# New statement order in the written-out front and end of a cross-attention layer on one core

## The chip, the cores and the metric

The kernel runs on one core of one Trainium2 chip. A core has five engines with an instruction queue each: TensorE (PE in the profile, its weight loads PEld), VectorE (DVE), ScalarE (ACT), GpSimd (POOL) and SyncE (SP), which issues most transfers. Each engine works through its own instructions in the order in which the program gives them, and waits where an operand or a buffer is not there yet. The metric is the device time of one execution in microseconds (us); lower is better.

## The reference

One transformer layer: 16-head cross attention of `x` (128 x 128 x 256) to a context of the same shape, a feed-forward part of width 1024 with relu, and a layer norm behind each. The mask is strict (`j < i`), and row 0 of the weights is set to 0.

```python
q = (query @ Wq + bq).reshape(b, s, N_HEADS, D_K).transpose(0, 2, 1, 3)
k = (key @ Wk + bk).reshape(b, s, N_HEADS, D_K).transpose(0, 2, 1, 3)
v = (values @ Wv + bv).reshape(b, s, N_HEADS, D_K).transpose(0, 2, 1, 3)
scores = jnp.einsum('bhqd,bhkd->bhqk', q, k) / jnp.sqrt(jnp.float32(D_K))
scores = jnp.where(allowed, scores, NEG_INF)
attn = jax.nn.softmax(scores, axis=-1)
attn = attn.at[:, :, 0, :].set(0.0)
ctx = jnp.einsum('bhqk,bhkd->bhqd', attn, v).transpose(0, 2, 1, 3).reshape(b, s, d)
x = layer_norm(query + ctx @ Wo + bo, ln1_g, ln1_b)
ffn = jax.nn.relu(x @ W1 + b1) @ W2 + b2
out = layer_norm(x + ffn, ln2_g, ln2_b)
```

## The kernel before

The 128 sequences are worked in 64 pairs, p = 0 to 63, 256 rows each. The order on every engine is that of the statements: a manual schedule, with no planner behind it. There are three parts:

- **The front**, lines 1863 to 2449: pairs 0 to 6 by statements of their own, then steps 7 and 8 with the keys of the regular step, written out one by one as `do("weigh", 8)` and so on.
- **The regular step**, line 2450: `for p in range(9, 61): step(p)`, 52 steps over one list of keys, `ORDER` (each key one small operation, some for an older pair), with `EMPTY` naming where PE is given empty instructions.
- **The end**, line 2453 on: steps 61 and 62 written out with the same keys, and a tail for pair 63 and all that is still open of 59 to 63.

A step interleaves several pairs: the scores and softmax of p, the projections of the next, the attention output of p-2 and the feed-forward part of p-3 and p-4. Large products are made from seven block products instead of eight; for that, `combine_weights` (L1105 to L1108, four POOL instructions) makes sums of weight blocks once (`wvt`, `wot`, `wqt`, `wkt`), and for the hidden layer of the last pairs `late(p).run(n)` (class `Hidden`, L1050) makes product n, with `xS` (POOL, L1646) the sums of its input's blocks.

Names that the steps below use:

- `mask` (L456, L464), `maximum` (DVE L475, then POOL L476 subtracts), `exponential` (ACT L483, in the regular step `eh`/`el` keys, L937), `sums` (DVE L498/L499, then POOL L500 normalises): the softmax, by high (`hi` = 1) and low half of the rows.
- `turn_on_pe` (PE L569, ACT L571) and `turn` with `bring_all` (DVE L533, then transfers L552): the weights turned for the product with the values, in the first pairs on PE, later by DVE and sixteen small transfers. `weigh` (PE L586, L596) is that product, `context` and `attention_out` (L635) follow it; `attention_sum` (DVE L683) adds the input, to which `add_bo` (POOL L295) has added a bias.
- `project_keys`, `project_queries` (PE L300), `copy_keys` (ACT L345); in the regular step queries and keys leave PSUM at ACT L1181 and L1219, values at L1265, L1278 and L1695.
- `hidden`, `second`, `second_sum` (DVE L904), `second_product` (L977), `sum_add` (L995): the feed-forward part. `residual1` (POOL L721, L724) prepares what `second_sum` adds.
- In the tail `scale_62` (DVE L1809) and `shift_62` (L1816, which needs POOL's deviation of L657/L658) make the output of pair 62; `last_part` (PE L1826, DVE L1834/L1835 or L1832), `last_scale` (L1839, L1840, POOL L1841), `last_shift` (L1845) and `last_out` (L1852, then a store) that of pair 63.

PSUM has eight banks, used by number, so a product can also wait for a bank to be read out.

Of the kernel before, what the change touches and what calls it, by code (L numbers as in the profile page):

```python
# [10 lines left out]
ALU = mybir.AluOpType  # L11
# [8 lines left out]
def tile_cross_attention_block(  # L20
# [1877 lines left out]
    mask(1, 1, B)  # L1898
    project_keys(2)
    add_bo(0)  # L1900
# [4 lines left out]
    maximum(1, 1, ONE)  # L1905
    scores(1, 0)
    exponential(1, 1, ONE)
    weigh(0)
    context(0)
    project_queries(2)  # L1910
    maximum(1, 1, TWO)
    mask(1, 0, A)
    mask(1, 0, B)
    maximum(1, 0, ALL)
    attention_out(0)
    copy_keys(2)
    exponential(1, 1, TWO)
    values(2)
    sums(1, 1, ONE)
    tokens(3, "c")  # L1920
    copy_queries(2)
    exponential(1, 0, ALL)
    scores(2, 1)
    attention_sum(0)
    stats(0, states[0]["t1"], 1)
    deviation(0, 1)
    stack_values(2)
    shift(0, 1)
# [21 lines left out]
    turn_on_pe(1, 1, range(3, 4))  # L1950
    tokens(3, "x")
    mask(2, 0, B)
    turn_on_pe(1, 0, range(0, 1))
    mask(2, 0, A)
    add_bo(1)
    maximum(2, 0, ALL)
# [44 lines left out]
    exponential(3, 1, TWO)  # L2001
    mask(3, 0, A)
    maximum(3, 0, ALL)
    second(0, 1)
    weigh(2)
    spread_values(3)
    context(2)
    second_sum(0)
    project_keys(4, 6)
    sums(3, 1, ONE)  # L2010
    exponential(3, 0, ALL)
    attention_out(2)
    scale_w1()
    copy_keys(4)
    sums(3, 1, TWO)
    sums(3, 0, ALL)
    project_queries(4)
    attention_sum(2)
# [31 lines left out]
    project_keys(5)  # L2050
    maximum(4, 1, TWO)
    exponential(4, 0, ALL)
    sums(4, 1, ONE)
    exponential(4, 1, TWO)
    sums(4, 0, ALL)
    sums(4, 1, TWO)
    second(1, 1)
    second_sum(1)
    hidden(2, range(2, 4), None, (2, 3, 4, 0))
    residual1(2)  # L2060
    turn(4, 0, 0)
    load_ahead(3)
    copy_keys(5)
    copy_queries(5)
# [12 lines left out]
    tokens(6, "c")
    mask_high(5, 2, 2)
    exponential_by_head(5, 1, range(8, 12), True)
    exponential_by_head(5, 1, range(12, 16), True)  # L2080
    mask(5, 0, A)
    project_queries(6)
    mask(5, 0, B)
    bring(4, nc.sync, LATE_FIRST)
    low_maximum(5)
    exponential_by_head(5, 0, range(8, 12), True)
    mask_high(5, 0, 1)
# [1015 lines left out]
```

## Time and profile before

| | us |
|---|---|
| runs | 1472.11, 1468.98, 1474.38; median 1472.11 |
| the profiled execution | 1469.98 |
| its span, first to last instruction | 1468.2 |
| mean granted TensorE clock | 0.997 |

All durations below come from the profiled execution. A line of its timeline has the start, the duration, the engine, the line of the kernel, the operation, output <- input and a count of equal instructions, and in brackets the idle time before it with what released it. Two numbers of PE overlap a little, since matmuls are pipelined; what a group takes is best read from its start to the start of the next.

### The profile page before, as it was taken

To read this page: it belongs to the slowest core of one execution; us is meant where nothing else is said; L and a number is where in the kernel's file an instruction comes from. 1 tells how busy PE (TensorE), PEld (TensorE's weight loads), DVE (VectorE), ACT (ScalarE), POOL (GpSimd) and SP (SyncE) were. 2 spreads that over 40 slices of the span, in tenths; PEclk is the share of its full clock that TensorE was granted. 3 is DMA by queue.
4 is the path that set the end of the run, shared out by engine and by line. 5 is a ranking of instruction groups with operands and counts; after the bars stand their busy time and mean duration, and the time that the engine had idled before them with its cause. 6 is when DMAs were issued, how large, how long until landed. Compare 5 with 4: busy or idle time off the path is not lost.

```text
span 1468.2 us, 62017 instructions
## 1 busy us (share of the span) xinstructions
PE 1447.0 (99%) x20713; PEld 1391.6 (95%) x20713; DVE 1371.9 (93%) x3175; ACT 1303.4 (89%) x5559; POOL 1271.2 (87%) x1872
## 2 busy tenths in 40 slices
PE   8999899999999999999999999999999999999998
PEld 7778799999999999999999999999999999999988
DVE  6987999999999999999999999999999999999767
ACT  5659899999999999999999999999999999999743
POOL 5986898988988988988988998998998998998966
PEclk9999999999999999999999999999999999999999
DMA  8274766766766766766766766766766776774541
GB/s 208 63 143 102 179 154 156 162 157 156 161 160 153 162 158 153 163 160 153 160 158 157 159 158 158 160 158 156 163 157 153 163 161 149 164 158 116 140 103 51
DMA packets 367881, 220.34 MB, mean 150 GB/s; under 512 B 280032, under 2 KB 335584, under 8 KB 367584
## 3 DMA queue, kind: packets, MB, share of 16 engines
q1 hardware_dynamic: 365296, 214.27, 63.8%
q8 instruction: 187, 3.06, 1.0%
q10 hardware_dynamic: 2288, 2.11, 0.7%
q14 instruction: 110, 0.90, 0.2%
HBM read 55.06 MB, written 18.09 MB: 50 GB/s over the span
## 4 chain that ended last, share of the span: by engine, by line
PE 92%; DVE 4%; POOL 1%; DMA 1%; ACT 1%; issue 1%; SPq 0%; DVEq 0%; ACTq 0%; POOLq 0%
PE banks L1153 48%; PE banks L1364 24%; PE banks L440 6%; PE banks L596 4%; PE banks L586 2%; PE banks L300 2%; PE banks L875 2%; PE banks L977 1%; PE banks L635 1%; PE banks L356 1%; DVE sm L464 1%; ACT sm L937 1%; DVE turned L533 1%; PE banks L1050 0%; PE banks L1412 0%
## 5 line engine op out<-in xcount | busy, mean ns | idle before, releaser
L937 ACT ACTIVATE sm<-banks,nmx 128x128 f32<-128x128 f32 x944 | 340.8, 396 | 17.9 <-DVE nmx L1568 14.7
L937 ACT ACTIVATE sm<-sm,nmx 128x64 f32<-128x64 f32 x944 | 325.2, 384 | 1.5 <-DVE nmx L926 1.5
L937 ACT ACTIVATION_READ_ACCUMULATOR sm<-banks,nmx 128x1 f32 x944 | 222.8, 236 | 0.0
L937 ACT ACTIVATION_READ_ACCUMULATOR sm<-sm,nmx 128x1 f32 x944 | 221.8, 235 | 0.0
L533 DVE STREAM_TRANSPOSE turned<-sm 128x1024 f32<-128x1024 f32 x186 | 217.0, 1214 | 3.3 <-DMA brought<-turned 1.8
L1153 PE MATMUL banks<-wt,hS 128*128 128x128 f32 x1344 | 177.7, 275 | 0.0
L1364 PE MATMUL banks<-xS,w1t 128*128 128x128 f32 x1344 | 177.2, 275 | 0.0
L1153 PEld LDWEIGHTS banks<-wt,hS 128*128 128x128 f32 x1344 | 163.6, 192 | 0.1
L1364 PEld LDWEIGHTS banks<-xS,w1t 128*128 128x128 f32 x1344 | 163.4, 192 | 0.0
L1568 DVE TENSOR_REDUCE nmx<-banks 128x4 f32<-128x512 f32 x224 | 152.3, 680 | 1.9
L1557 POOL TENSOR_TENSOR hS<-hT 128x512 f32<-128x512 f32 x116 | 148.2, 1279 | 3.7 <-ACT hT L882 2.4
L1364 PE MATMUL banks<-brought,w 128*128 128x128 f32 x896 | 118.2, 275 | 0.0
L1153 PE MATMUL banks<-w,hT 128*128 128x128 f32 x896 | 109.8, 275 | 0.0
L1364 PEld LDWEIGHTS banks<-brought,w 128*128 128x128 f32 x896 | 109.0, 192 | 0.0
L1618 POOL TENSOR_TENSOR x1b<-x,g_r 128x512 f32<-128x512 f32 x56 | 72.4, 1293 | 39.4 <-ACT x L709 39.4
L1153 PEld LDWEIGHTS banks<-w,hT 128*128 128x128 f32 x896 | 104.8, 192 | 0.1
L440 PE MATMUL banks<-kT,qT 32*64 32x128 f32 (+1 forms) x3840 | 98.3, 331 | 1.8 <-ACT vz L1278 1.5
L1393 ACT ACTIVATE hT<-hT,b1e_c 128x256 f32<-128x256 f32 x224 | 95.7, 510 | 1.2 <-DVE hT L1389 1.1
L1562 DVE TENSOR_TENSOR banks<-banks,neg 128x256 f32<-128x256 f32 x224 | 93.3, 417 | 0.0
L440 PEld LDWEIGHTS banks<-kT,qT 32*64 32x64 f32 x3840 | 79.4, 131 | 12.6 <-ACT vz L1278 1.9
L709 ACT ACTIVATE x<-t,nb,sd 128x256 f32<-128x256 f32 x126 | 68.4, 593 | 19.7 <-POOL nb L732 12.9
L1219 ACT ACTIVATE kr<-banks,b_c 128x128 f32<-128x128 f32 x224 | 83.7, 411 | 1.7 <-PE banks L1153 1.7
(324 smaller groups left out, 4821.5 us busy)
## 6 DMA issues: line engine op xcount, KB each, us to landing
brought<-turned SPq DMA_DIRECT2D x936, 128.0 KB, 2.4
out_dram<-t SPq DMA_DIRECT2D x63, 256.0 KB, 4.0
xb<-in_x_dram SPq DMA_DIRECT2D x124, 128.0 KB, 3.2
cb<-in_ctx_dram SPq DMA_DIRECT2D x124, 128.0 KB, 3.2
x<-in_x_dram SPq DMA_DIRECT2D x56, 256.0 KB, 2.8
kT<-kr SPq DMA_DIRECT2D x112, 128.0 KB, 2.2
brought<-turned SPq DMA_DIRECT2D x40, 96.0 KB, 2.4
w<-in_L_xattn_W_dram SPq DMA_DIRECT2D x2, 1024.0 KB, 7.4
```

Of the source, the lines that this page charges most:

```text
L440: nc.tensor.matmul(st["sps", hi][r][s * HP : (s + 1) * HP, m * 2 * n : (m + 1) * 2 * n].rearrange("p (e j) -> p e j", e=2), st["qT"][strip ...
L533: nc.vector.transpose(turned[:, :, at : at + 256].rearrange("p j (n a) -> p n j a", a=32), states[p]["sm", hi].rearrange("p h j -> p (h j) ...
L709: nc.scalar.activation(x1[:, s], t1[:, s], AF.Identity, bias=st["nb", 1][:, s], scale=sd[:, s])
L937: nc.scalar.activation(sm[:, h, :], src, AF.Exp, bias=nmx[:, h : h + 1], scale=1.0, **({"accum_out": st["su"][:, at : at + 1]} if summed e ...
L1153: nc.tensor.matmul(out, left(k) if self.depth > 1 else left, right(k) if self.depth > 1 else right, start=(n == 1 and k == 0), stop=(k == ...
L1219: nc.scalar.activation(self.k[:, m, s * P : (s + 1) * P], src, AF.Identity, bias=bk_c[:, m : m + 1], scale=1.0,)
L1364: nc.tensor.matmul(ps[:, i * P : (i + 1) * P].rearrange("p (n a) -> p n a", a=32), left(i), right, start=(n in (1, 2, 5) and i == 0), stop ...
L1393: nc.scalar.activation(self.hT[:, f, at], self.hT[:, f, at] if src is None else src, AF.Relu, bias=b1e_c[:, f : f + 1], scale=1.0,)
L1557: engine.tensor_tensor(c[:, n], left, right, how)
L1562: nc.vector.tensor_tensor(ps[:, :, HP:], ps[:, :, HP:], neg[:, 1, None, :].to_broadcast([P, 4, HP]), ALU.add)
L1568: nc.vector.tensor_reduce(states[p]["nmx", 1][:, 4 * b : 4 * b + 4], banks[:, b].rearrange("p (n j) -> p n j", j=P), AX.X, ALU.max, negate ...
L1618: nc.gpsimd.tensor_tensor(st["x1b"], st["x1b"] if n else st["x1"], (be1b_r if n else g1_r)[:, None, :].to_broadcast([P, 2, D]), ALU.add if ...
```

## The change

Only the order of statements changes: every instruction of before has its counterpart, on the same engine and with the same operands. The front and the end are in a new order on all five engines; `ORDER`, `EMPTY` and the loop stay as they are.

POOL in the front. This is what stood between the first subtractions of pair 2's softmax (`sm_705`) and pair 1's bias (`x_80` is the tokens of pairs 0 and 1, `x_140` those of pairs 2 and 3):

```order
L476 TENSOR_TENSOR sm_705<-sm_705,nmx_2_706 128x1024
L295 TENSOR_TENSOR x_80<-x_80,bov_r 128x512
L476 TENSOR_TENSOR sm_705<-sm_705,nmx_2_842 128x1024
L500 TENSOR_TENSOR sm_705<-sm_705,rs_2_8_862 128x1024
L500 TENSOR_TENSOR sm_705<-sm_705,rs_2_0_873 128x1024
L500 TENSOR_TENSOR sm_705<-sm_705,rs_2_0_910 128x1024
L295 TENSOR_TENSOR x_140<-x_140,bov_r 128x512
```

And this is the same place now, from the second instruction of the first combination on (`sm_708` is the softmax of pair 2):

```order
L1106 TENSOR_TENSOR wqt<-wq,wqt 128x128
L1107 TENSOR_TENSOR wqt<-wq 128x128
L1108 TENSOR_TENSOR wqt<-wq,wqt 128x128
L500 TENSOR_TENSOR sm_708<-sm_708,rs_2_8_945 128x1024
L500 TENSOR_TENSOR sm_708<-sm_708,rs_2_0_950 128x1024
L500 TENSOR_TENSOR sm_708<-sm_708,rs_2_0_962 128x1024
L1105 TENSOR_TENSOR wkt<-wk 128x128
L1106 TENSOR_TENSOR wkt<-wk,wkt 128x128
L1107 TENSOR_TENSOR wkt<-wk 128x128
L1108 TENSOR_TENSOR wkt<-wk,wkt 128x128
L295 TENSOR_TENSOR x_140<-x_140,bov_r 128x512
L295 TENSOR_TENSOR x_80<-x_80,bov_r 128x512
```

Two combinations have come in, and the second addition to `x_80`, `add_bo(1)`, stands behind both and behind pair 2's normalisation. The combinations of `wv` and `wo` are now POOL's first work on data.

PE in the end, ahead of `weigh(63)` (L586 on `vd_180`), with the second half of pair 60's feed-forward part (L977) and pair 61's hidden layer (L1050), before:

```order
L977 MATMUL banks<-w_138,hT 128x128 x4
L977 MATMUL banks<-wt,hT 128x128 x4
L977 MATMUL banks<-wt,hS_27635 128x128 x4
L977 MATMUL banks<-w_138,hS_27635 128x128 x4
L1050 MATMUL banks<-cb_61_27511,w_132 128x128 x4
L586 MATMUL banks<-brought,vd_180 32x64 x8
L596 MATMUL banks<-brought,vz_178 32x64 x16
```

and now:

```order
L977 MATMUL banks<-wt,hS_27648 128x128 x12
L1050 MATMUL banks<-xS_27591,w1t 128x128 x4
L977 MATMUL banks<-w_138,hT 128x128 x4
L977 MATMUL banks<-wt,hT 128x128 x4
L977 MATMUL banks<-w_138,hS_27648 128x128 x4
L1050 MATMUL banks<-xS_27591,w_132 128x128 x4
L586 MATMUL banks<-brought,vd_180 32x64 x8
L596 MATMUL banks<-brought,vz_178 32x64 x16
```

Two products on `xS`, numbers 6 and 3, came in ahead of `weigh(63)`; number 1, the L1050 on `cb_61`, went ahead of all these rows. The profile counts two matmuls for each of the order's here, eight for x4.

DVE in the tail, from `scale_62` on, before:

```order
L1809 SCALAR_TENSOR_TENSOR t_62_28043<-t_62_28043,mv_62_28074,g_r 128x256 x2
L1834 TENSOR_TENSOR t_last<-banks,x1b_27947 128x256
L1835 BN_STATS bs_last<-t_last 128x6
L1816 SCALAR_TENSOR_TENSOR t_62_28043<-t_62_28043,sd_62_28082,be_r 128x256
L1834 TENSOR_TENSOR t_last<-banks,x1b_27947 128x128
L1835 BN_STATS bs_last<-t_last 128x6
L1816 SCALAR_TENSOR_TENSOR t_62_28043<-t_62_28043,sd_62_28082,be_r 128x256
L1839 BN_AGGR mv_last<-bs_last 128x2
L1840 TENSOR_SCALAR sd_last<-mv_last 128x1
L1845 SCALAR_TENSOR_TENSOR t_last<-t_last,mv_last,g_r 128x256
L1832 BN_STATS bs_last<-banks 128x6
```

and now:

```order
L1809 SCALAR_TENSOR_TENSOR t_62_28022<-t_62_28022,mv_62_28059,g_r 128x256 x2
L1816 SCALAR_TENSOR_TENSOR t_62_28022<-t_62_28022,sd_62_28082,be_r 128x256 x2
L1834 TENSOR_TENSOR t_last<-banks,x1b_27973 128x256
L1835 BN_STATS bs_last<-t_last 128x6
L1839 BN_AGGR mv_last<-bs_last 128x2
L1840 TENSOR_SCALAR sd_last<-mv_last 128x1
L1845 SCALAR_TENSOR_TENSOR t_last<-t_last,mv_last,g_r 128x256
L1852 SCALAR_TENSOR_TENSOR t_last<-t_last,sd_last,be_r 128x256
L1834 TENSOR_TENSOR t_last<-banks,x1b_27973 128x128
```

Both `shift_62` now follow `scale_62` directly, and the first row's output (L1852) follows its L1845 directly. The store of pair 62 moves ahead of the last two.

The diff, cut to these places:

```diff
     tokens(2, "x")
+    combine_weights(wv, wvt)
+    combine_weights(wo, wot)
     scores(0, 1)
...
     project_keys(2)
-    add_bo(0)
+    copy_keys(2)
     turn_on_pe(0, 1, range(2, 3))
...
     mask(1, 0, A)
-    mask(1, 0, B)
-    maximum(1, 0, ALL)
-    attention_out(0)
-    copy_keys(2)
...
+    mask(2, 1, A)
     deviation(0, 1)
-    stack_values(2)
+    turn_on_pe(1, 1, range(0, 1))
     shift(0, 1)
     norm1(0)
+    maximum(1, 0, ALL)
...
+    combine_weights(wq, wqt)
...
+    sums(2, 0, ALL)
+    combine_weights(wk, wkt)
...
+    add_bo(1)
+    mask(3, 1, A)
...
-    project_queries(6)
...
+    project_keys(6)
...
+    project_queries(6)
...
-    combine_weights(wk, wkt)
...
-    combine_weights(wo, wot)
...
-    combine_weights(wq, wqt)
...
-    combine_weights(wv, wvt)
...
+    do("q4", 7)
+    do("qr", 7)
+    do("kr", 7)
...
+    do("el4", 7)
+    do("eh1", 7)
...
+    do("vr", 7)
+    do("br1", 7)
+    do("weigh", 8)
...
-    do("q4", 7)
-    do("kr", 7)
-    do("eh0", 7)
-    do("qr", 7)
-    do("weigh", 8)
...
+    late(61).run(6)
...
+    combine_x1_one(61, 2)
+    late(61).run(3)
+    weigh(63)
...
+    scale_62(0)
+    finish_shift(61)
+    store(61)
+    late(63).relu(6)
+    scale_62(1)
+    deviation(62, 2)
+    shift_62(0)
+    shift_62(1)
+    late(63).relu(5)
+    late(63).relu(4)
+    last_part(0, 0, D)
+    store(62)
+    last_scale(0, 1)
+    last_shift(0)
+    last_out(0)
+    last_part(1, 0, P)
+    last_part(1, 1, P)
```

In step 7 the last part of pair 8's queries, `qr`, had four of pair 7's sixteen exponential keys behind it (`eh1`, `el4`, `el3`, `el7`); now it has eight (`el4`, `eh1`, `eh0`, `eh2`, `el3`, `el1`, `el2`, `el6`).

More of the change, by code (lines that the diff above doesn't have):

```diff
@@ L1950, in tile_cross_attention_block @@
[L1950 to L1956, printed above, removed]
+    keep_b1(ps_b1)
+    scores(2, 0)
+    mask(2, 0, B)
+    exponential(2, 1, TWO)
+    mask(2, 0, A)
+    turn_on_pe(1, 1, range(2, 3))
+    exponential(2, 1, ONE)
+    maximum(2, 0, ALL)
+    hidden(0, range(0, 2), None, (2, 3, 4, 0))
+    hidden(0, range(2, 4), None, (2, 3, 4, 0))
+    combine_weights(wq, wqt)
+    turn_on_pe(1, 1, range(3, 4))
@@ L1992, in tile_cross_attention_block @@
     maximum(3, 1, ONE)
+    second(0, 0, pad=3)
+    second(0, 1)
     stack_values(3)
-    scores(3, 0)
-    tokens(5, "x")
+    maximum(3, 1, TWO)
+    exponential(3, 1, TWO)
+    bring(2, nc.sync, EVERY[:8])
+    weigh(2)
     mask(3, 0, B)
-    exponential(3, 1, ONE)
+    mask(3, 0, A)
+    maximum(3, 0, ALL)
     norm1(1)
@@ L2000, in tile_cross_attention_block @@
     turn_x1(1)
[L2001 to L2006, printed above, removed]
+    second_sum(0)
+    stats(0, states[0]["t2"], 2)
+    project_keys(4, 6)
+    exponential(3, 1, ONE)
+    sums(3, 1, ONE)
+    add_bo(2)
+    tokens(5, "x")
+    load_ahead(4)
+    nc.gpsimd.tensor_tensor(b1e_c, b1e_c, b1_c, ALU.add)
+    load_ahead(5)
+    project_queries(4)
+    exponential(3, 0, ALL)
+    sums(3, 0, ALL)
     context(2)
-    second_sum(0)
@@ L2049, in tile_cross_attention_block @@
+    tokens(8, "x")
+    project_keys(5)
+    copy_keys(5)
+    sums(4, 1, ONE)
+    exponential(4, 0, ALL)
+    sums(4, 0, ALL)
     second(1, 0, pad=3)
[L2050 to L2053, printed above, removed]
+    second(1, 1)
     exponential(4, 1, TWO)
-    sums(4, 0, ALL)
     sums(4, 1, TWO)
-    second(1, 1)
-    second_sum(1)
[L2059 to L2064, printed above, removed]
@@ L2151, in tile_cross_attention_block @@
     exponential_by_head(6, 0, range(8, 12), True)
[L2152 to L2155 removed]
     second_half(2, 1)
+    turn_x1_blocks(4)
+    do("weigh", 7)
+    do("context", 7)
     exponential_by_head(6, 0, range(0, 4), True)
[L2158 to L2160 removed]
+    copy_keys(7)
+    do("res0", 7)
+    do("oc2", 7)
+    hidden(3, range(2, 4), None, (2, 3, 4, 6))
+    load_ahead(6)
+    turn(6, 1, 1)
```

1678 lines of the change are left out of this document (819 added, 859 removed).

## The prediction

> **What bounds the kernel now.** I read the page's busy times first, then stretches of the span, then what TensorE waited for in the stretches where it is not full.
>
> ```profile
> PE 1447.0 (99%) x20713; PEld 1391.6 (95%) x20713; DVE 1371.9 (93%) x3175; ACT 1303.4 (89%) x5559; POOL 1271.2 (87%) x1872
> ```
>
> TensorE (PE) is busy 1447.0 of 1468.2 us. The change neither adds nor takes away a matmul, so what it can gain is at most the 21.2 us in which PE stands, plus what a slowed clock costs. Where they lie is in the stretches (columns: stretch, its length, busy us and instructions of PE, PEld, DVE, ACT, POOL, granted clock, DMA share, GB/s):
>
> ```profile
> 0.00:60.00 60.00, 55.61 (x611) 44.49 (x615) 45.61 (x80) 39.85 (x78) 41.87 (x40) 0.97 0.53 129
> 60.00:120.00 60.00, 58.19 (x635) 48.64 (x624) 54.06 (x85) 34.03 (x106) 45.79 (x44) 1.00 0.66 142
> 120.00:200.00 80.00, 74.62 (x1069) 67.48 (x1069) 70.48 (x158) 73.45 (x335) 67.41 (x107) 1.00 0.64 147
> 200.00:1320.00 1120.00, 1120.00 (x16727) 1097.67 (x16726) 1086.22 (x2600) 1063.01 (x4692) 1003.29 (x1530) 1.00 0.70 158
> 1320.00:1400.00 80.00, 79.64 (x1078) 77.19 (x1077) 69.42 (x162) 68.98 (x289) 69.49 (x96) 1.00 0.49 120
> 1400.00:1470.00 70.00, 58.98 (x617) 56.11 (x615) 46.15 (x96) 24.13 (x66) 43.31 (x60) 0.95 0.29 80
> ```
>
> From 200 to 1320 us, which is the regular step, PE is busy 1120.00 of 1120.00: a lead or a lag that the front hands to step 9 is carried through, neither won back nor lost. So the change is worth the shift at the entry of the loop plus the shift behind it. PE idles 4.4, 1.8 and 5.4 us in the three front stretches, 0.4 in the next to last and 11.0 in the last, a window that reaches 1.8 us beyond the span; 3.6 of these 11.0 are the last two waits below, and most of the rest lies behind its last matmul. The longest waits there (line, what it waited for, us in all, times, longest):
>
> ```profile
> PE banks L300 <- DVE sm L464: 1.1, 1, 1.1
> ...
> PE banks L586 <- ACT qT L1181: 1.4, 1, 1.4
> PE banks L440 <- ACT vz L1278: 1.1, 1, 1.1
> ...
> PE banks L586 <- DMA x1t<-xb: 3.1, 1, 3.1
> PE banks L1050 <- POOL xS L1646: 0.5, 1, 0.5
> ```
>
> **The change, front.** All four `combine_weights` move ahead. Each is four POOL instructions:
>
> ```profile
> 19.99 5.61 POOL L476 TENSOR_TENSOR sm<-sm,nmx 128x1024 f32<-128x1024 f32 x3 [14.86 <-DVE nmx L475]
> ...
> 51.79 1.28 POOL L295 TENSOR_TENSOR x<-x,bov_r 128x512 f32<-128x512 f32 x1
> ...
> 54.94 3.75 POOL L500 TENSOR_TENSOR sm<-sm,rs 128x1024 f32<-128x1024 f32 x2
> ...
> 115.72 0.23 POOL L657 TENSOR_SCALAR ve<-mv 128x2 f32<-128x2 f32 x1 [10.26 <-DVE mv L651]
> ...
> 119.01 0.46 POOL L1105 TENSOR_TENSOR wkt<-wk 128x128 f32<-128x128 f32 x1
> ```
>
> 4 x 0.46 less overlaps is about 1.75 us a combination. `wv` and `wo` go into POOL's wait of 14.86 us before 19.99 and cost nothing; without that cover they would cost 3.5 us. `wq` and `wk` leave a POOL that had just waited 10.26 us and go between the softmax work of pair 2, 3.5 us together. Behind them stands `add_bo(1)`, the L295 of 51.79. It also falls behind four more passes over pair 2's weights (L476 and L500, 1.9 us each by the 3.75 of two) and another addition (1.28): 3.5 + 7.5 + 1.3 = 12.3 us. The low heads of pair 1, whose maximum on DVE now comes behind the masks of pair 2, hold POOL up by up to 2.8 us more. So it starts at 64 to 67 instead of 51.79 and ends at about 67; then these are late:
>
> ```profile
> 63.54 0.68 DVE L683 TENSOR_TENSOR t<-banks,x 128x512 f32<-128x512 f32 x1
> ...
> 73.92 0.68 DVE L904 TENSOR_TENSOR t<-banks,x1b 128x512 f32<-128x512 f32 x1
> ...
> 74.66 1.99 PE L300 MATMUL banks<-cT,wk 128*128 128x256 f32 x8 [0.39 <-DVE t L904]
> ```
>
> `attention_sum(1)` (L683) moves from 63.54 to about 67. The DVE work from there to `second_sum(0)` (L904) was 10.4 us and is 8.4 in the new order, so L904 starts at 75.3 to 76.3 instead of 73.92, and the keys of pair 4 on PE are 1.3 to 2.2 us late. Another delay lies ahead of it and is swallowed by it:
>
> ```profile
> 36.51 1.94 ACT L345 ACTIVATE kT<-banks,bkh,half 128x256 f32<-128x256 f32 x4
> ```
>
> `copy_keys(2)` now stands ahead of the copies of the turned blocks, so `weigh(0)` starts some 1.3 us later. Of the lag, part goes into the later wait L300 <- DVE sm (1.1 us), but in its place PE now asks for the keys of pair 6 ahead of its queries, into a bank that four exponentials have to leave first. I carry +1.3 us (0 to +3) to step 7.
>
> Steps 7 and 8 give back:
>
> ```profile
> 146.77 1.71 PE L440 MATMUL banks<-kT,qT 32*64 32x128 f32 x64
> ...
> 160.18 0.55 PE L586 MATMUL banks<-brought,vd 128*32 128x64 f32 x16 [1.43 <-ACT qT L1181]
> ...
> 161.19 0.66 PE L596 MATMUL banks<-brought,vz 128*32 128x64 f32 x32
> 163.00 1.60 PE L440 MATMUL banks<-kT,qT 32*64 32x128 f32 x64 [1.15 <-ACT vz L1278]
> ...
> 160.00:170.00 10.00, 8.06 (x199) 7.39 (x200) 9.87 (x17) 8.25 (x39) 8.31 (x14) 1.00 0.76 218
> ```
>
> PE waits 1.43 us for ACT's last queries of pair 8 and 1.15 for its values. The new order takes some 3 us of exponentials from in front of the first and some 4 from in front of the second, so both waits, 2.6 us, can go. What is late next is DVE: it is busy 9.87 of 10 us there, and the mask of pair 8 comes after as much work as before. I take 1.6 of the 2.6. **Front: +1.3 - 1.6 = -0.3 us, from -3 (both waits and half a microsecond more, no lag left) to +3 (the lag of the two combinations, nothing given back).**
>
> **The end.** In steps 61 and 62 DVE gets about 1 us more work ahead of the scores of pairs 62 and 63; DVE is free for 10.6 of 80 us there, so I take **+0.5 (0 to +1.5)**. Then comes the one long stop:
>
> ```profile
> 1407.16 8.33 SPq L552 DMA_DIRECT2D brought<-turned  x8
> ...
> 1413.53 1.06 PE L977 MATMUL banks<-w,hS 128*128 128x128 f32 x8
> 1414.42 1.06 PE L1050 MATMUL banks<-cb,w 128*128 128x128 f32 x8
> 1415.41 0.32 PE L586 MATMUL banks<-brought,vd 128*32 128x64 f32 x8
> 1418.83 0.32 PE L586 MATMUL banks<-brought,vd 128*32 128x64 f32 x8 [3.11 <-DMA x1t<-xb]
> ...
> 1421.20 2.63 PE L1050 MATMUL banks<-xS,w1t 128*128 128x128 f32 x16
> 1423.67 1.89 PE L635 MATMUL banks<-wo,cxT 128*128 128x256 f32 x8
> ...
> 1420.00:1430.00 10.00, 10.00 (x114) 9.62 (x106) 5.69 (x13) 0.98 (x2) 2.31 (x8) 0.88 0.17 54
> ```
>
> `weigh(63)` (L586) needs the turned weights of pair 63, whose issues keep SP until 1415.49; the last piece lands at 1418.83. The label x1t is only the transfer that the trace saw last. The new order puts two more groups of L1050 products ahead of it, at 0.89 us each (from 1413.53 to 1414.42): PE comes 1.8 us later. The turning of pair 63 on DVE has 1.1 us less work ahead of it, and with the lag of steps 61 and 62 I let the data land 0.5 us earlier. The stop becomes 3.1 - 1.8 - 0.5 = 0.8, a gain of 2.3. Behind the stop the rows are slow: from 1418.83 to 1421.20, 2.37 us for what takes about 1.5 at 160.18 to 161.85 (1.67 for all of it, while here the first eight were done before the stop); from 1421.20 to 1423.67, 2.47 us for sixteen products that take 1.78 at 0.89 for eight. That is 0.87 + 0.69, or 1.5 us, with a granted clock of 0.88 in the stretch. After stops of 1.43 and 1.15 us (160.18, 163.00) the rows show no slowing (L440 x64: 1.60 against 1.71), so I let it go with the stop. POOL's wait before xS of pair 63 (0.5) goes as well, because POOL now does pair 62's part and two outputs while it used to stand; against this DVE, which has 21.9 us of work between the sum of pair 63 and the last hidden sums, beside 22.5 of PE, holds PE up by some 0.8. **Stop: -2.3 - 1.5 - 0.5 + 0.8 = -3.5 (-5.3 to 0).**
>
> [...]
>
> **The tail** costs:
>
> ```profile
> 1458.70 0.88 DVE L1809 SCALAR_TENSOR_TENSOR t<-t,mv,g_r 128x256 f32<-128x256 f32 x2
> 1459.50 0.42 DVE L1834 TENSOR_TENSOR t_last<-banks,x1b 128x256 f32<-128x256 f32 x1
> ...
> 1462.72 0.15 DVE L1840 TENSOR_SCALAR sd_last<-mv_last 128x1 f32<-128x1 f32 x1
> 1462.79 0.47 DVE L1845 SCALAR_TENSOR_TENSOR t_last<-t_last,mv_last,g_r 128x256 f32<-128x256 f32 x1
> ...
> 1463.82 0.47 DVE L1852 SCALAR_TENSOR_TENSOR t_last<-t_last,sd_last,be_r 128x256 f32<-128x256 f32 x1
> ...
> 1459.35 0.81 POOL L658 TENSOR_TENSOR sd<-ve,power 128x2 f32<-128x2 f32 x1
> ```
>
> DVE is full from 1458.70 to its last result because last_part and the last statistics lie between each deviation and its use. In the new order `shift_62` (L1816) follows L1809 at once: DVE is free at 1459.50, POOL's deviation ends at 1460.16, 0.65 us of standing. L1852 follows L1845 at once: from L1840 to L1852 it took 1.10 us, of which only 0.46 are now filled, 0.64 more; for the second half some 0.4. Together 1.7. The store of pair 62 leaves earlier, so the last store has the queue to itself, for which I take 0.4 off. **Tail: +1.3 (0 to +1.7).**
>
> **Sum.** -0.3 + 0.5 - 3.5 + 1.3 = -2.0 us. The profiled execution took 1469.98 us, so 1468.0 for it. It lies 2.1 us under the median of the runs, 1472.11, so the forecast is 1470.1.
>
> **Rivals.**
> 1. *The POOL lag stays (slower).* The two combinations hold POOL 3.5 us where the sum of pair 1 waits for it; if DVE, full at 160 to 170, is what ends steps 7 and 8, nothing is given back, and a full PE carries +3.5 through the loop. For it: the 9.87. Against: PE waits for ACT there, not for DVE. With +0.5 and +1.3 and the stop's -3.5 that is +1.8, 1473.9; should the lag also meet an unshortened stop, +5.3, 1477.4. It decides from 2.3 us of lag at step 9 on. Chance 0.18.
> 2. *The stop stays.* If the turned weights of pair 63 land 1.8 us later, with steps 61 and 62, PE's two groups are only put before the same stop, and the clock falls as before: -0.3 + 0.5 + 0 + 1.3 = +1.5, 1473.6. Against: less DVE work ahead of the turning. Chance 0.12.
> 3. *The slow rows are not the stop's.* Then 1.5 remains lost: -0.5, 1471.6. Chance 0.11. [...]
> 4. *More is won.* No lag reaches step 7 and the waits there go (-3), the stop and its clock go whole (-5.3), the tail's +1.3 is half hidden (+0.2): -8.1, 1464.0. Against: three favourable ends at once. Chance 0.17.
>
> My forecast has 0.42. Taking each unknown from end to end gives -8.3 to +6.2, 1463.8 to 1478.3; the range that leaves out under 2 in 10 is 1464 to 1477. A measurement of this kernel can tell about 0.5%, 7.4 us, from no change. Rival 4 alone is faster by more: 0.17. Slower by more takes the upper end of rival 1 with an entry worse than any term here: 0.10. Within: 0.73.
>
> **What would show it.** Right: PE's keys of pair 4 at 76 to 77 us; L586 of pair 8 without a wait for qT; PE full in 200 to 1320; the wait L586 <- DMA near 0.8 us and a granted clock over 0.95 in the ten microseconds behind it; DVE standing before L1816 and L1852. Wrong: the loop entered over 3 us earlier or later, or a new wait of over 2 us in steps 61 and 62, which I have priced from DVE's free time only.

## The result and the profile after

| | before | after |
|---|---|---|
| runs, median | 1471.42 us (1468.98 to 1474.38, 4 runs) | 1490.93 us (1488.22 to 1491.16, 4 runs) |
| ratio, 95% interval | | 1.0131 [1.0113, 1.0148] |
| span of the profiled execution | 1468.2 | 1486.4 |

The forecast was 1470.1 us with a range of 1464 to 1477; the kernel takes 19.5 us more than before. The stretches of after, with the columns of the prediction's first such view, the middle stretch the same:

```profile
0.00:60.00 60.00, 52.79 (x607) 40.87 (x608) 43.71 (x77) 35.82 (x70) 43.56 (x49) 0.97 0.64 140
60.00:120.00 60.00, 56.02 (x602) 46.64 (x601) 54.49 (x82) 34.81 (x90) 52.98 (x50) 1.00 0.53 121
120.00:200.00 80.00, 70.44 (x990) 62.16 (x989) 63.36 (x134) 66.65 (x301) 47.39 (x75) 0.98 0.55 128
200.00:1320.00 1120.00, 1120.00 (x16726) 1097.58 (x16725) 1086.21 (x2600) 1063.06 (x4692) 1003.89 (x1530) 1.00 0.70 158
1320.00:1420.00 100.00, 95.00 (x1195) 89.42 (x1192) 81.09 (x191) 82.76 (x360) 80.98 (x114) 1.00 0.50 121
```

The loop is as full as before (1120.00 of 1120.00), so nothing is won back in it. The three front stretches together have PE busy 179.25 us where they had 188.42. What the front does not lose is lost behind the loop.

How much is lost by which point is read from a row that both kernels have, here the first scores product (L440) of a pair. Before and after, that of pair 8, and those of pairs 62 and 63:

```profile
163.00 1.60 PE L440 MATMUL banks<-kT,qT 32*64 32x128 f32 x64 [1.15 <-ACT vz L1278]
...
1350.86 1.68 PE L440 MATMUL banks<-kT,qT 32*64 32x128 f32 x64
...
1386.25 1.83 PE L440 MATMUL banks<-kT,qT 32*64 32x128 f32 x64 [0.35 <-ACT vz L1278]
```

```profile
168.80 1.91 PE L440 MATMUL banks<-kT,qT 32*64 32x128 f32 x64 [0.72 <-ACT sm L937]
...
1364.51 2.29 PE L440 MATMUL banks<-kT,qT 32*64 32x128 f32 x64
...
1403.13 1.12 PE L440 MATMUL banks<-kT,qT 32*64 32x128 f32 x32
```

Pair 8 is 5.80 us late, pair 62 13.65, pair 63 16.88. The same difference for all points that matter here, for after and for the experiments (us against the profile of before; time is the median against that of before on the same chip; f1, f2 and f3 ran once, k1, k2 and k3 twice). One of the four executions of e2 took 3649.76 us at a clock of 1.00, for no cause that the record shows, and is left out of its time here.

| kernel | pair 4 | 6 | 7 | 8 | 9 | 61 | 62 | 63 | time |
|---|---|---|---|---|---|---|---|---|---|
| after | 4.29 | 6.16 | 6.42 | 5.80 | 11.49 | 11.60 | 13.65 | 16.88 | +19.5 |
| e1_front | 4.86 | 6.98 | 7.24 | 6.69 | 11.93 | 12.03 | 12.04 | 12.78 | +12.4 |
| e2_end | -1.46 | -1.47 | -1.45 | -1.45 | -1.43 | -1.40 | 0.66 | 3.90 | +6.6 |
| e3_early_front | 5.72 | 7.72 | 7.97 | 7.89 | 7.94 | 8.73 | 8.73 | 9.09 | +8.9 |
| e4_steps_7_8 | -0.22 | -0.23 | -0.25 | -1.28 | 4.04 | 4.26 | 4.27 | 4.69 | +5.8 |
| f1_combine | 5.35 | 8.74 | 8.99 | 8.37 | 13.75 | 13.95 | 13.95 | 13.95 | +15.1 |
| f2_pair1 | 8.77 | 9.24 | 9.50 | 8.88 | 14.50 | 14.71 | 14.71 | 14.71 | +14.8 |
| f3_bank_add | 4.97 | 5.53 | 5.79 | 5.17 | 9.82 | 9.97 | 9.98 | 9.99 | +10.9 |
| h1_steps_61_62 | 0.05 | 0.04 | 0.03 | 0.00 | 1.04 | 1.17 | 3.20 | 6.43 | +6.8 |
| h2_tail | -0.62 | -0.63 | -0.65 | -0.66 | -0.62 | -0.39 | -0.39 | 0.03 | +0.2 |
| i1_tail_moved | -0.48 | -0.50 | -0.52 | -0.54 | -0.48 | -0.42 | -0.43 | 0.46 | -2.0 |
| i3_joins | -0.09 | -0.09 | -0.09 | -0.08 | 1.03 | 1.06 | 3.10 | 6.37 | +6.1 |
| k1_dve_before | -0.21 | -0.23 | -0.25 | -0.26 | -0.24 | -0.21 | 10.43 | 39.30 | +42.2 |
| k2_dve_new | 1.16 | 1.14 | 1.12 | 1.10 | 2.13 | 2.17 | 13.16 | 35.40 | +36.8 |
| k3_front_dve_before | -0.65 | -0.66 | -0.69 | 1.27 | 14.28 | 14.70 | 14.70 | 14.70 | +15.4 |

**The front.** What PE waited for from 28 to 212 us, after (line, what it waited for, us in all, times, longest):

```profile
PE banks L1153 <- DVE sm L464: 3.2, 1, 3.2
PE banks L300 <- ACT sm L937: 3.1, 1, 3.1
PE banks L569 <- ACT hT L882: 1.7, 1, 1.7
PE banks L1153 <- ACT vz L1696: 1.3, 1, 1.3
PE banks L569 <- ACT brought L571: 1.3, 1, 1.3
PE banks L586 <- DMA brought<-turned: 1.1, 1, 1.1
...
PE banks L300 <- DVE t L904: 0.7, 1, 0.7
```

The two waits of before on `qT` (1.43) and `vz` L1278 (1.15) are gone, as the prediction had it, and others stand in their place. The first on this list lies behind the scores of pair 8 (the timelines of DVE and PE and one stretch, after; ahead of them DVE's row of before):

```profile
164.20 0.42 DVE L464 TENSOR_TENSOR sm<-banks,neg 128x256 f32<-128x256 f32 x1
```

```profile
169.92 1.23 DVE L533 STREAM_TRANSPOSE turned<-sm 128x1024 f32<-128x1024 f32 x1
171.08 0.40 DVE L1562 TENSOR_TENSOR banks<-banks,neg 128x256 f32<-128x256 f32 x1
171.51 0.69 DVE L1568 TENSOR_REDUCE nmx<-banks 128x4 f32<-128x512 f32 x1
172.12 1.24 DVE L533 STREAM_TRANSPOSE turned<-sm 128x1024 f32<-128x1024 f32 x1
173.39 0.42 DVE L464 TENSOR_TENSOR sm<-banks,neg 128x256 f32<-128x256 f32 x1
...
173.87 0.71 PE L1153 MATMUL banks<-wv,cT 128*128 128x128 f32 x4 [3.15 <-DVE sm L464]
...
174.64 1.85 PE L1153 MATMUL banks<-w,hT 128*128 128x128 f32 x8
176.28 1.91 PE L1153 MATMUL banks<-wt,hS 128*128 128x128 f32 x8
...
174.00:180.00 6.00, 6.00 (x40) 6.00 (x41) 5.07 (x10) 4.42 (x16) 2.35 (x2) 0.72 0.29 66
```

DVE turns weights of pair 7 and masks and reduces another part of pair 8's scores (L1562, L1568) before it comes to the mask that PE's bank waits for, and PE waits 3.15 us. In before the mask began 1.20 us after the scores (164.20 against 163.00), now 4.59 after (173.39 against 168.80). Behind the stop the clock is 0.72 for six microseconds; eight products that take 0.89 take 1.64 (from 174.64 to 176.28).

**The end.** What PE waited for from 1335 us on, after; and the rows around the stop of `weigh(63)`:

```profile
PE banks L977 <- DVE t L985: 2.3, 1, 2.3
PE banks L1050 <- DVE t L995: 1.9, 1, 1.9
PE banks L1153 <- DVE t L1299: 1.9, 4, 1.0
...
1437.48 0.65 PE L586 MATMUL banks<-brought,vd 128*32 128x64 f32 x16
...
1439.28 2.05 PE L1050 MATMUL banks<-xS,w1t 128*128 128x128 f32 x16
1441.17 1.89 PE L635 MATMUL banks<-wo,cxT 128*128 128x256 f32 x8
...
1440.00:1450.00 10.00, 9.69 (x77) 9.09 (x76) 6.27 (x13) 3.87 (x9) 9.30 (x17) 1.00 0.16 50
```

The 3.11 us on the turned weights are gone, and so are the slow rows behind them: sixteen L1050 take 1.89 (from 1439.28 to 1441.17) where they took 2.47, at a clock of 1.00. But ahead of the stop and behind it PE now waits for DVE, because of what DVE has in its queue before the sums that free PE's bank:

```profile
1413.27 1.23 DVE L920 TENSOR_REDUCE nmx<-banks 128x8 f32<-128x1024 f32 x1
1414.41 0.68 DVE L985 TENSOR_TENSOR t<-x1b,banks 128x512 f32<-128x512 f32 x1
...
1415.24 1.13 PE L977 MATMUL banks<-wt,hS 128*128 128x128 f32 x8 [2.28 <-DVE t L985]
...
1458.16 1.46 DVE L995 TENSOR_TENSOR t<-t,banks 128x384 f32<-128x384 f32 x3
...
1459.67 1.16 PE L1050 MATMUL banks<-sm_own,w1t 128*128 128x128 f32 x8 [1.92 <-DVE t L995]
```

### The profile page after: what moved, and what is told of

Read it like the earlier page. It is cut to its first block, busy times and chain, and to the rows that moved or that the text cites. A ratio compares the mean times of both kernels' runs of the same rounds, so it can differ in the third digit from the quotient of the medians.

```text
span 1486.4 us, 62015 instructions
## 1 busy us (share of the span) xinstructions
PE 1452.5 (98%) x20713; PEld 1391.8 (94%) x20713; DVE 1374.7 (92%) x3175; ACT 1304.7 (88%) x5559; POOL 1271.9 (86%) x1872
## 4 chain that ended last, share of the span: by engine, by line
PE 87%; DVE 4%; POOL 3%; ACT 2%; issue 1%; DMA 1%; SPq 1%; POOLq 0%; ACTq 0%; DVEq 0%
PE banks L1153 46%; PE banks L1364 23%; PE banks L440 6%; PE banks L596 4%; PE banks L586 2%; PE banks L875 2%; PE banks L300 1%; ACT sm L937 1%; POOL hS L1557 1%; SPq L552 1%; PE banks L977 1%; PE banks L1050 0%; PE banks L356 0%; PE banks L894 0%; PE banks L1412 0%
## 5 line engine op out<-in xcount | busy, mean ns | idle before, releaser
L1568 DVE TENSOR_REDUCE nmx<-banks 128x4 f32<-128x512 f32 x224 | 152.7, 682 | 2.0
L440 PE MATMUL banks<-kT,qT 32*64 32x128 f32 (+1 forms) x3840 | 99.0, 331 | 1.1 <-ACT sm L937 0.7
L1562 DVE TENSOR_TENSOR banks<-banks,neg 128x256 f32<-128x256 f32 x224 | 93.3, 417 | 0.0
L440 PEld LDWEIGHTS banks<-kT,qT 32*64 32x64 f32 x3840 | 79.6, 131 | 12.1 <-ACT sm L937 0.9
L764 POOL TENSOR_TENSOR t<-t,g_r 128x512 f32<-128x512 f32 x62 | 79.5, 1283 | 5.8 <-ACT t L746 5.8
```

Source lines behind the costliest of these rows:

```text
L440: nc.tensor.matmul(st["sps", hi][r][s * HP : (s + 1) * HP, m * 2 * n : (m + 1) * 2 * n].rearrange("p (e j) -> p e j", e=2), st["qT"][strip ...
L764: nc.gpsimd.tensor_tensor(t2, t2, g2_r[:, None, :].to_broadcast([P, 2, D]), ALU.mult)
L1562: nc.vector.tensor_tensor(ps[:, :, HP:], ps[:, :, HP:], neg[:, 1, None, :].to_broadcast([P, 4, HP]), ALU.add)
L1568: nc.vector.tensor_reduce(states[p]["nmx", 1][:, 4 * b : 4 * b + 4], banks[:, b].rearrange("p (n j) -> p n j", j=P), AX.X, ALU.max, negate ...
```

## The experiments

All are built from statements of the two kernels. Unless a line says otherwise, each computes the whole layer.

**Which part costs what: e1 to e4.** The new front with the old end, the old front with the new end, the new order only up to the scores of pair 7, and only behind them. (In step 8 one group of PE's empty instructions has 2 instead of 5 in the new order, so three of before have no counterpart; this goes with the new step 8 in e1 and e4.)

```diff
 e1_front against the changed kernel: the end as before
-    do("re2", 59)
+    do("xs0", 60)
+    do("xs1", 60)
...
 e4_steps_7_8 against the kernel before: from the scores of pair 7 to the loop as in the change
-    do("scores", 7)
-    turn(6, 1, 0)
...
+    combine_c(7)
+    store(0)
+    turn(6, 1, 0)
...
```

> New front, old end. Theory A (each part loses by itself): the loop is entered 11.5 us later than before, as in the changed kernel, and the old end neither adds nor returns anything: +11.5 us, 1.0078 of before. Theory B (the end loses because it is reached late): the same entry, and another 2 to 6 us lost in the old end: +14 to +18.

> Old front, new end. Theory A: the end by itself costs what the two traces differ by behind the loop, +6.7 us (1.0045): about +5.8 in steps 61 and 62, +2.6 before the weights of pair 62, -4.4 at the stop of pair 63, +2.4 behind it. Theory B: the new end costs under 2 us when it is entered on time.

> New order up to the scores of step 7, then the old order of what is left, old end. If steps 7 and 8 lose by their own order, this is the lag that the trace shows at the scores of step 7: +6.4 us, or up to 2 less if the old steps 7 and 8 have slack. If steps 7 and 8 lose only because POOL and DVE reach them late, it is +10 to +12.

> Old order up to the scores of step 7, then the new order of steps 7 and 8, old end. If their own order loses: +5 us. If they lose only because of what reaches them late: 0 to +1. My prediction had -1.6 for them.

Medians: 1482.69 us, ratio 1.0087 [1.0071, 1.0102]; 1476.91, 1.0054 [1.0037, 1.0071]; 1479.16, 1.0063 [1.0046, 1.0080]; 1476.09, 1.0038 [1.0023, 1.0053]; before 1470.30. Front and end alone, +12.4 and +6.6, make 19.0 beside the +19.5 of both, as theory A had it for each (+11.5 and +6.7). Within the front, pairs 0 to 6 alone hand on 7.97 us, and the old steps 7 and 8 behind them neither add nor give back (7.94 at pair 9). That is more than the 6.4 that was expected, and the time (+8.9) lies between the two forecasts; e1 and e3 have a slow clock near 115 us, 0.91 on the mean from 110 to 130 us in both and 0.83 from 110 to 120 us in e1, where after has 1.00. Steps 7 and 8 alone add 4.3 (from -0.25 to 4.04), with a wait on L464 of 2.4 us and, behind their stops, a clock of 0.67 from 160 to 170 us. The two halves make 11.98 at pair 9, where e1 has 11.93. So the losses are separate and add up; none is the echo of another.

How much of the loss of steps 7 and 8 is standing and how much is clock differs. From the scores of pair 7 to those of pair 9, PE is busy 34.11 of 39.49 us in before. In e4 it is busy 37.68 of 43.78, so it stands only 0.7 us more, and by an estimate 3.4 of the 4.3 us are the slow clock (0.92 on the mean of the 43.78 us). In e1 it is busy 35.21 of 44.18 at a clock of 1.00: the same steps add 4.7 us there, 3.6 of them standing.

**Inside pairs 0 to 6 and step 8: f1, f2, f3**, each against e1_front and each run once, so that their times have no interval.

```diff
 f1_combine: two combinations back on their old place
-    combine_weights(wq, wqt)
-    combine_weights(wk, wkt)
...
+    combine_weights(wq, wqt)
+    combine_weights(wk, wkt)
     do("weigh", 7)
 f2_pair1: pair 1's low half and the keys' copy earlier
-    copy_keys(2)
...
+    copy_keys(2)
...
+    maximum(1, 0, ALL)
+    exponential(1, 0, ALL)
+    sums(1, 0, ALL)
 f3_bank_add: mask and queries ahead of the keys of pair 6; three statements of step 8 behind its masks
+    mask(5, 0, A)
+    project_queries(6)
...
+    do("add3", 8)
+    do("max3", 8)
+    do("eh6", 8)
```

> New front, old end, but the combinations of wq and wk (3.5 us of POOL) go back behind the softmax of the early pairs, ahead of the weights of step 7. If POOL's 3.5 us are what makes the front late (rival 1 of the prediction), the keys of pair 4 come 2 us or more earlier and the lag at the scores of step 9 falls from 11.9 us to 9 or less. If the lag is a sum of small waits on ACT and DVE, the keys of pair 4 come under 1 us earlier and the lag at step 9 stays above 11.

> New front, old end, but pair 1's low maximum, exponential and sums go back ahead of pair 2's masks, and the copies of pair 2's keys back behind the weights of pair 0. The two waits that the trace has for them, 1.3 us (L569 for ACT's copy L571 at 33 us) and 1.7 us (L569 for ACT L882 at 54 us), should go; if they simply add to the rest, the lag at step 9 falls from 11.9 to about 9. If later waits take their place, it stays above 11.

> New front, old end; (a) the queries of pair 6, with the mask that frees their bank, go ahead of the keys again: the wait of 2.8 us behind the scores of pair 5 becomes about 1.1, as before; (b) in step 8 the last block's mask addition and maximum (1.0 us of DVE) go behind the masks of the low rows: the wait of 3.2 us for DVE behind the scores of step 8 becomes about 2.2. Together the lag at step 9 falls from 11.9 to about 9.2. If ACT's late exponentials set the turn ahead of those masks, (b) changes nothing.

f1 (1485.45 us, before 1470.31) is no faster than e1. The keys of pair 4 do not come earlier (79.23 us where e1 has 78.71), and the wait on L904, which the late `add_bo(1)` should cause, only goes from 0.7 to 0.5: POOL's two combinations are not the loss. (That f1 is 2.8 us above e1 goes with a clock of 0.83 in 110 to 130 and in 170 to 180 us, where e1 has 0.91 and 1.00; see the last section.) f2 (1485.12) is no faster either. Its edit removes both of its waits, on `hT` and on L571, and gets two new ones (PE's waits from 28 to 215 us of f2, and the stretch behind the first):

```profile
PE banks L268 <- ACT x L709: 3.3, 1, 3.3
...
PE banks L411 <- ACT qT L326: 1.1, 1, 1.1
...
50.00:60.00 10.00, 9.93 (x71) 7.90 (x71) 7.96 (x12) 8.27 (x18) 8.63 (x8) 0.70 0.34 50
```

With a clock of 0.70 on the mean of ten microseconds the new stop costs, by an estimate from these two numbers, about 3 us more than its length. What f2 was to measure, the price of the late low half, stays open. f3 (1481.22) is 1.5 us below the median of e1, which is at the lower edge of e1's own executions (1481.26 to 1483.88), and 2.1 better at pair 9. Both of its edits act on the waits that they aim at (its waits, same stretch):

```profile
PE banks L1153 <- DVE sm L464: 2.4, 1, 2.4
...
PE banks L586 <- DMA brought<-turned: 1.5, 1, 1.5
...
PE banks L300 <- ACT sm L937: 1.0, 1, 1.0
```

The keys of pair 6 wait 1.0 instead of 2.8 us for the exponentials to leave their bank, of which the next `weigh` takes some back, waiting 1.5 for its transfers; the mask of pair 8 is awaited 2.4 instead of 3.2. What stays of their 2.6 us is 1.5 up to pair 6 and 0.7 over steps 7 and 8. The 1.5 is nearly all clock, 0.83 in e1 from 110 to 120 us and 1.00 in f3: between the scores of pairs 4 and 6 PE stands 2.8 us in e1 and 2.6 in f3. And f2, which has e1's order there without the slow stretch, loses even less between these two points (9.24 less 8.77, or 0.5 us) than f3 (0.6). So the order of bank use is not shown to be a cause. Over steps 7 and 8 both clocks are 1.00 and the 0.7 is standing: the operations ahead of the mask are a small cause, by one execution.

**Steps 61 and 62: h1, i3, k1, k2.**

```diff
 h1_steps_61_62 against before: new order up to the scores of pair 63
+    do("re2", 59)
+    do("re3", 59)
+    do("xs2", 60)
...
 i3_joins against h1: a product and its sum earlier, two sums behind masks
+    do("w3", 61)
...
+    do("wb", 61)
...
     do("maskA1", 62)
+    do("wb", 60)
+    do("ro1", 60)
 k1_dve_before against h1: DVE's statements in the old order
-    do("add2", 61)
-    do("max2", 61)
...
+    do("max1", 61)
+    do("ok", 61)
+    do("add3", 61)
...
 k2_dve_new against before: DVE's statements in the new order
+    do("maskA0", 61)
...
+    do("v2", 61)
+    do("add2", 61)
+    do("maskB", 61)
...
```

> Old front, new order of steps 61 and 62 up to the scores of pair 63, then the old order of what is left. If their own order loses: +5.3 us at the scores of pair 63, +5 at the end (1.0035). If they lose only together with the new tail (the bank and buffer orders of the two), under +2.

> Old front, new steps 61 and 62, old order behind the scores of pair 63, as in the kernel with only those two steps; and the product w3 of step 61 stands before h4, its sum wb on DVE ahead of the turns of pair 62, and the sums ro1 and wb of step 60 behind the first two masks of pair 62. All is computed. Theory A (single sums on DVE that stand behind turns or ahead of masks hold PE's next bank): the waits L1153 <- DVE t L1299 (1.05) and of the values of pair 62 on the mask (about 0.6) go, so 1.4 to 1.9 us less than the kernel with only steps 61 and 62 (which was +5.3 over these steps): +3.4 to +3.9. Theory B (DVE's 97% load makes the lag, wherever its single instructions stand): the next waits take it back, +4.8 to +5.5 over these steps.

> Old front, new steps 61 and 62 on PE, ACT, POOL and SP but with DVE's statements in the order of before wherever no operand forbids it; old order behind. All is computed. New steps alone lost 5.3 us between the first scores of step 61 and the scores of pair 63. Theory A (DVE's order makes the loss): at most 1.5 us are lost there. Theory B (PE's order asks for banks and operands sooner than any DVE order can give them): 4 us or more are lost.

> Old front, old steps 61 and 62 on PE, ACT, POOL and SP, with DVE's statements in the new order wherever no operand forbids it; old order behind. All is computed. Theory A (DVE's order makes the loss): 4 us or more are lost between the scores of pairs 61 and 63. Theory B (the order of the other engines): at most 1.5 us. If both this and the kernel with the old DVE order lose, the loss lies in the mismatch of two orders, and neither engine's alone.

h1: 1477.10 us, ratio 1.0042 [1.0028, 1.0056], 2.03 us lost in step 61 and 3.23 in step 62, as in after. Only some 2 of these 5.3 us are waits that the profile lists. From the scores of pair 61 to those of pair 63, after has PE standing 2.3 us (60.36 busy of 62.69) and before 0.35 (57.06 of 57.41), at a clock of 1.00 in both; the other 3.3 are a longer busy time for the same products, spread over many places (the scores of pair 62 above take 2.29 instead of 1.68). i3 (1476.77, 1.0040 [1.0024, 1.0055]): in it `wb` and `ro1` of step 60 come too late for what they read and feed, so the outputs of pairs 56 and 57 are changed, against its expectation; every operation and its shape is there. The wait of 1.05 us on L1299 is gone, and PE's waits from 1326 to 1400 us begin with

```profile
PE banks L1153 <- DVE t L1299: 1.0, 4, 0.3
PE banks L1153 <- ACT hT L1405: 0.7, 1, 0.7
```

and 5.31 us are lost (1.06 to 6.37) where h1 loses 5.26. The next waits took it back, as theory B had it; that DVE's load is the reason is not shown. k1 and k2 were to say whose order makes the loss: 1512.12 us, ratio 1.0281 [1.0252, 1.0311], and 1506.74, 1.0245 [1.0215, 1.0275]. Beside its own partners DVE's old order loses nothing here and its new one 5.3 us; beside those of the other kernel they lose 39.5 and 33.2 us in two steps. Part of that is clock again, 0.91 and 0.92 on the mean of these steps; PE stands 26.1 and 23.2 us in them. DVE's waits from 1328 to 1428 us in k1, and from 1328 to 1388 in before:

```profile
DVE t L1299 <- PE banks L1153: 41.0, 10, 11.5
```

```profile
DVE t L1299 <- PE banks L1153: 4.9, 7, 1.1
```

The reading that fits is that DVE stands at the head of its queue for a product that PE has far behind, while the operand that PE wants stands behind the same instruction. This was the third outcome of the expectation: a mismatch of two orders, and neither engine's alone. But these are not pure exchanges. Where an operand forbade the old place, statements of the other engines moved too: of the 80 statements with PE's products there, 18 stand elsewhere in k1 than in h1, and 17 elsewhere in k2 than in before. What part of the loss is theirs is not shown.

**The same for steps 7 and 8: k3**, against e4.

```diff
-    do("add2", 7)
-    do("max2", 7)
     do("maskA1", 7)
     do("lowmax", 7)
+    do("add2", 7)
...
+    do("max2", 7)
```

> Old pairs 0 to 6, new steps 7 and 8 on PE, ACT, POOL and SP, with DVE's statements of steps 7 and 8 in the order of before wherever no operand forbids it; old end. All is computed. New steps 7 and 8 alone handed the loop a lag 5.4 us larger than they took. Theory A (the turns that DVE has ahead of the masks of pair 8): at most 2.5 us, and the wait of PE on the mask is under 1.2 us. Theory B (ACT's exponentials and POOL make it): 4.5 us or more.

1485.37 us, 1.0100 [1.0070, 1.0129]; 15.0 us are lost from pair 7 to pair 9, against 4.3 in e4. Of these, by an estimate 8.5 are slow clock (0.84 on the mean of 54.46 us), and PE stands 6.4 us more than before (busy 42.64 of 54.46). Theory A falls as stated: giving DVE its old order makes it worse, although the wait on the mask is shorter (1.9). That ACT and POOL make it, theory B, is not shown by this either; k3 keeps the five empty instructions, and 7 of PE's 49 statements there stand elsewhere than in e4.

**The tail: h2 and i1.**

```diff
 h2_tail against before: new order behind the scores of pair 63
+    do("ro0", 62)
+    bring_all(62, EVERY[0:4])
...
 i1_tail_moved against h2
     attention_sum(61)
+    first_of_seven(59)
...
     second_product(61, 6)
+    sum_add(61, 1)
+    sum_add(61, 2)
+    sum_add(61, 3)
```

> Old front, old order up to the scores of pair 63, new order from there to the end. All is computed. Theory A (the terms of the end are separate): the stop of weigh(63) goes with its clock loss, -4.4 us; in its place come the wait L977 <- DVE t L985 ahead of weigh(62), +2.6, and the wait L1050 <- DVE t L995, +2.4; the last rows +0.2. Sum about +0.8 us against before, and both waits are there with 2.0 to 2.6 and 1.5 to 2.2 us. Theory B (the waits L985 and L995 come from the lag of steps 61 and 62): both waits are under 1 us, and the kernel is 3 to 5 us faster than before.

> As the kernel with only the new tail, but L985 (first_of_seven of pair 59) stands on DVE behind the attention sum of pair 61 instead of behind the last mask and maximum of pair 63, and the three L995 of pair 61 directly behind the last of its hidden sums instead of behind three sums of pair 62. All is computed. Theory A (DVE's order makes both waits): the wait on L985 falls from 2.3 to under 0.3 us and that on L995 from 1.9 to under 0.6, so 4 us less than the kernel with only the new tail, 3 to 4.5 us faster than before. Theory B (DVE's amount of work makes them): the time comes back as waits on the mask, on u3 or on the hidden sums of pair 62, and it stays within 1.5 us of the kernel with only the new tail.

h2: 1470.88 us, ratio 1.0004 [0.9995, 1.0014] against 1470.69. The stop is gone, and the waits on L985 and L995 are there with 2.3 and 1.9 us, without any lag ahead of them, as theory A had it: they belong to the tail's own order. i1: 1468.71 us, 0.9988 [0.9979, 0.9997], 2.0 us faster than before and 2.2 faster than h2. Its waits from 1380 us on:

```profile
PE banks L977 <- DVE t L985: 1.0, 1, 1.0
```

The wait on L995 is gone; that on L985 has fallen to 1.0 instead of under 0.3, and a few small ones of 0.2 to 0.3 came. About half of the 4 us of theory A came true. i1 is the one version here that beats both kernels, by 0.12%.

## Why the prediction was wrong

| term | forecast | measured |
|---|---|---|
| front, at pair 9 | -0.3 | +11.5 |
| steps 61 and 62, at pair 63 | +0.5 | +5.3 |
| from there to `weigh(63)`, L985 among it | 0 | +3.3 |
| stop of `weigh(63)`, clock | -3.8 | -4.4 |
| behind it, L995 among it | +0.3 | +2.2 |
| tail | +1.3 | +0.2 |

The last column adds up to 18.1; the spans differ by 18.2. Its four last rows come from PE's rows: a start less the work that PE has ahead of it, against before. The forecast's -3.5 is split as it was worked: -2.3 and -1.5 for stop and clock, -0.5 and +0.8 behind.

- **The front's -0.3 failed, in two steps.** *Pairs 0 to 6* were carried with +1.3 (0 to +3) and gave 6.4 at the scores of pair 7. Of the two delays followed in detail, the weighing of pair 0 did wait 1.3. The other came out in its first number alone: `add_bo(1)` ended at 66.76 where 67 was said, but DVE did not wait for it. The sum that needs it followed at 67.81 in DVE's own queue, which had last stood before 64.79, for PE's scores; and in f1, where the addition ends at 65.85, the sum comes no earlier (68.96). That the 67 fitted was luck:

```profile
67.81 0.65 DVE L683 TENSOR_TENSOR t<-banks,x 128x512 f32<-128x512 f32 x1
...
64.26 2.50 POOL L295 TENSOR_TENSOR x<-x,bov_r 128x512 f32<-128x512 f32 x2
```

The keys of pair 4 came at 78.33, 3.7 late and not 1.3 to 2.2. And I let the second delay be "swallowed" by the first and part of the lag go into later waits. None was swallowed. Up to the scores of pair 7 PE stands 12.9 us where it stood 6.2, with nearly the same busy time (140.31 and 140.57): 1.3 (L571), 1.7 (`hT` of `hidden`, not foreseen: the late low half of pair 1 stands ahead of it on ACT), 0.7 (L904), 3.1 at the keys of pair 6 (I named this bank and gave it no price; before loses 1.4 between the scores of pairs 5 and 6), 1.1 on transfers, and smaller ones. *Steps 7 and 8* were to give 1.6 back and cost 5.1. I wrote that "the mask of pair 8 comes after as much work as before", having counted DVE's work and not when its parts can start. The waits on ACT did go; ahead of the mask DVE is then late by 3.4 us, and the slow clock behind that stop adds an estimated 1.7 (six microseconds at 0.72).
- **Rival 1 named the right engine and the wrong cause.** It said that DVE, 9.87 of 10 us busy, ends steps 7 and 8, and gave +3.5. DVE does hold up step 8, but POOL's combinations do not make the lag (f1), and steps 7 and 8 cost 4.3 without any lag (e4).
- **Steps 61 and 62, +0.5, failed**, as the prediction feared of a term "priced from DVE's free time only". DVE does have 1.2 us more work between the scores of pairs 61 and 62. But in step 62 it is busy *less* than before (27.0 us against 28.5 from pair 62 to pair 63) and the step is 3.2 us longer: it stands in turn with PE. Free time in a stretch says nothing on whether each operand is ready at its place. The sign of failure that I had named, a new wait of over 2 us, did not come, for the longest is 1.0: the loss is many small ones. Which pair of statements makes it is open: of single waits, the one removed came back elsewhere.
- **The stop was right, and a little more than said**: 2.8 of its 3.1 us and the 1.5 of the clock went. Of rival 2 (the stop stays) nothing is seen here, and rival 3 (the slow rows are not the stop's) holds in one profile only: of the twelve with the old end, e3's alone has the same stop without slow rows behind it (last section); by the table of the kernels and the spans of their profiled executions it takes, from the scores of pair 63 to the end, 1.1 us less than before, the other ten 0.2 to 3.2 more. So the 1.5 stands behind this stop in most of these profiles, not in each.
- **Behind and ahead of the stop two waits were missed.** "DVE holds PE up by some 0.8" was the right mechanism without its place: the sums L985 and L995, each the reader that frees PE's next bank, stand on DVE behind work that this bank does not need. In i1, where they are moved ahead of some of it, the waits of 2.3 and 1.9 us fall to 1.0 and nothing.
- **The tail**: DVE stands 0.61 us before L1816 and 0.44 and 0.18 before L1852, where 0.65, 0.64 and 0.4 were said; with the shorter last store (2.68 us from the end of L1852 to the end of the span, before 2.80) only 0.2 remain:

```profile
1478.00 0.88 DVE L1816 SCALAR_TENSOR_TENSOR t<-t,sd,be_r 128x256 f32<-128x256 f32 x2 [0.61 <-POOL sd L658]
...
1480.91 0.48 DVE L1852 SCALAR_TENSOR_TENSOR t_last<-t_last,sd_last,be_r 128x256 f32<-128x256 f32 x1 [0.44 <-POOL sd_last L1841]
```

The range missed because its ends were those of the terms I had priced. That a reordering of all rows makes waits at places not looked at had no term, and these are the larger part of the 18 us.

## What to carry to other kernels

In this front the stops on PE added up; net two of them only where the same wait swallows both. Price a reordering by going through the bound engine's waits one by one (who frees this bank, and what stands ahead of that reader in its queue), not by an engine's free time in a stretch: k1 and k2 lost 33 to 40 us in two steps with DVE's order taken from one schedule and most of the rest from another that loses 0 or 5. And a repair of one wait is worth only what the next wait leaves, 0 in i3 and half in i1. A difference between two profiles is to be split into standing and slow clock before it is given a cause: in f3 most of the apparent gain at pair 6 was clock (0.83 from 110 to 120 us in e1, 1.00 in f3).

## What was not expected of the hardware

Of stops of about the same length, one is followed by a slow clock and another is not. In before, the stops of 1.43 and 1.15 us at 160 and 163 us left the clock at 1.00, from which I concluded that such stops cost nothing more. h1 has the same statements there and the same stop:

```profile
160.19 0.67 PE L586 MATMUL banks<-brought,vd 128*32 128x64 f32 x16 [1.42 <-ACT qT L1181]
160.62 1.10 PE L596 MATMUL banks<-brought,vz 128*32 128x64 f32 x32
...
160.00:170.00 10.00, 8.38 (x191) 7.67 (x192) 9.01 (x15) 7.29 (x34) 7.33 (x13) 0.83 0.68 197
```

The products take 0.67 and 1.10 us instead of 0.55 and 0.66, the clock is 0.83 on the mean of the ten microseconds where before has 1.00, a wait of 0.91 on the mask follows, and h1 enters the loop 1.04 us late, though its statements up to there are those of before. In after, behind the stop of 3.14 us that ends at 114.82 the clock is 1.00 (to 125 us), and behind that of 3.15 us that ends at 173.87 it is 0.72 (174 to 180 us). In e3 the stop of `weigh(63)` is 3.54 us long, longer than in before, and the sixteen products behind it take 1.89 us (from 1429.71 to 1431.60), not 2.47:

```profile
1428.35 0.32 PE L586 MATMUL banks<-brought,vd 128*32 128x64 f32 x8 [3.54 <-DMA x1t<-xb]
...
1429.71 2.05 PE L1050 MATMUL banks<-xS,w1t 128*128 128x128 f32 x16
```

Taken in finer stretches, the 0.72 in after is one stretch at half the clock: 0.50 from 174.71 to 178.12 us, 1.00 from 170.72 to 174.71 and again from 178.12 us on. In before, the slow rows behind the stop of `weigh(63)`, which ends at 1418.83, have a stretch of the same length, 0.50 from 1419.03 to 1422.44 us, with 1.00 on both sides. Why one stop is followed by such a stretch and another is not, these profiles do not show. Length alone does not tell: a stop of 1.42 us, with short ones beside it, was followed by slowing in h1, and one of 3.54 us in e3 was not. For reading such profiles: here differences of 1 to 3 us went with the clock (the 1.04 us of h1 above, the 2.8 of f1 against e1), so a stop's price has to be read with the granted clock behind it.
